# A graph attention layer: high softmax planes on ScalarE, weight remainders on GpSimd in quarters, q2 stacks straight from PSUM, five planes and a later value product

## The chip, the cores and the metric

The kernel runs on one core of a Trainium2 chip, in one launch. The metric is the device time of one execution in microseconds. Three executions of the kernel before gave a median of 329.63 us (328.7 to 329.89); one more was profiled. TensorE is called PE here, VectorE DVE, ScalarE ACT, GpSimd POOL and SyncE SP, as in the profile.

## The reference

```python
h = relu(layernorm(x))                       # x: 384 x 1024
q, k, v = h @ wq.T + bq, h @ wk.T + bk, h @ wv.T + bv
q2, k2, v2 = q @ wiq.T + biq, k @ wik.T + bik, v @ wiv.T + biv   # 16 heads of 64
scores = q2 @ k2.T / 8 + mask                # per head 384 x 384, mask from 6528 edges
attn = softmax(scores)
out = x + (attn @ v2).reshape(384, 1024) @ wo.T + bo
```

All is float32. The mask holds a weight by edge type where there is an edge, the weight of the fourth type on the diagonal where there is none, and minus infinity elsewhere.

## The kernel before, in words

**Numbers in two parts.** A value is held as a high part (rounded to the matrix format by a copy on ACT or DVE) and a remainder (value minus high part). A product is three matmuls, high by high, high by remainder, remainder by high (`mm3`, lines 373 to 375). A chunk of a weight matrix is a tile `raw` of 128 x 1024, loaded by SP (`load`, line 68); `split_hi` (line 80) writes its high part into `whl`, `split_lo` (line 85) the remainder, on DVE or POOL.

**Stages.** To about 150 us: layernorm, the projections v, q, v2 (kept as three bf16 parts in `vhl`) and k, and beside them the edge mask, gathered in `ma`. From about 161 us: the attention loop. It has a step `i` for each block of 128 queries of each head, so three steps for a head and six for a pair of heads `p`; 48 steps give scores, and some more finish. Two generators fill PE's time between: `fill_qk` computes q2 and k2 of the next pairs (16 chunks of 24 matmuls), `fill_o` the output projection. `fill` hands them out by a credit of 7.9 or 8 per step, with 84 ahead of the loop.

**A step.** Everything is issued in the order in which it is written, on each engine in its queue (the order is manual). Step `i` issues in this order: half of the filling; `do_S(i)`, two matmuls into a score bank `s` (two banks); the other half; `do_ttr(i - 1)` on DVE (line 721), which adds the mask, writes `e` and the row's minimum of the negated scores, and so frees the bank; `do_low(i - 4)`; `do_exp(i - 2)` on ACT (line 725) with the row sum; `do_norm(i - 3)`; every third step the value product `do_A` (line 750, nine matmuls) `LA` + 2 steps behind the head's first scores; a step later `do_ao` (lines 760 and 761), and once per pair `do_aos` (lines 765 and 766); last the tasks of the filling (`qk_head`: load, split and evacuation of chunks).

**The softmax planes.** The normalized row, scaled by 32768, becomes two fp16 planes in a tile `pl`. `do_norm` computes the reciprocal of the sum on DVE (line 729), the factor (line 730) and the high plane (line 732) on POOL. `do_low` computes the low plane on DVE (line 737) from `e`, the factor and the high plane, and then issues one transposing DMA from SP (line 742) into `pt`, where `do_A` reads it. There are three `pl` tiles, five `e` tiles, and room for four heads in `pt`.

**q2 and k2 stacks.** `qk_done` evacuates a finished chunk: ACT writes the high part into `nat` (line 383), DVE the remainder (line 384). For the scores, a head's high and remainder are stacked on 128 partitions: four DMAs copy 64-partition parts from `nat` into `qs` (lines 570 to 573) for q2, four into `ks` (line 580) for k2. All come from SP except in the first pair, where ACT issues half of them.

**Weight remainders.** In `qk_head` POOL takes the odd chunks and DVE the even ones; in `wo_prep`, which prepares the last six output chunks, POOL takes four (`OPOOL`) and DVE two.

Of the kernel before, what the change touches and what calls it, by code (L numbers as in the profile page):

```python
# [8 lines left out]
F32 = mybir.dt.float32  # L9
F32R = mybir.dt.float32r  # L10
I32 = mybir.dt.int32
F16 = mybir.dt.float16
BF16 = mybir.dt.bfloat16
PSC = 32768.0
AF = mybir.ActivationFunctionType
OP = mybir.AluOpType

N, D, NT, KT, NP = 384, 1024, 3, 8, 8
# [7 lines left out]
def gnn_kernel(ctx: ExitStack, tc: tile.TileContext, x, edges, erows, etw, wq, wk, wv, wiq, wik, wiv, wo,  # L26
# [6 lines left out]
    nc = tc.nc  # L33
    const = ctx.enter_context(tc.tile_pool(name="const", bufs=1))
    big = ctx.enter_context(tc.tile_pool(name="big", bufs=1))
    wpool = ctx.enter_context(tc.tile_pool(name="wpool", bufs=4))
    work = ctx.enter_context(tc.tile_pool(name="work", bufs=2))
# [1 line left out]
    dram = ctx.enter_context(tc.tile_pool(name="dram", bufs=1, space=bass.MemoryType.DRAM))  # L39
    ctx.enter_context(tc.manual_schedule())  # L40

    EB = 5
    NTAB, RNG = 3, EC // 3
    JI = [0, 1, 3, 5, 8, 11, 14, RNG]
    WARM = (20, 6, 0)
# [4 lines left out]
    def gtile(tag):  # L50
        return big.tile([128, 2, KT, N], F32R, tag=tag, name=tag)
# [8 lines left out]
    raw, whl = {}, {}  # L60
# [18 lines left out]
        else:  # L79
            nc.scalar.activation(dst[0], raw[w], AF.Copy)  # L80

    def split_lo(w, eng=None):
        if w < NCH:
            hi, lo = whl[w]
            (eng or nc.vector).tensor_tensor(lo, raw[w], hi.bitcast(F32), OP.subtract)  # L85

    def split(w, lo_eng=None, dst=None, hi_dve=False):
        split_hi(w, dst, hi_dve)
        split_lo(w, lo_eng)


    G3 = gtile("g3")
# [2 lines left out]
    xn = [xall[:, (NT + t) * D:(NT + t + 1) * D] for t in range(NT)]  # L95
    ert = work.tile([128, N], F32, tag="e", name="er", bufs=EB)
    er = ert[:, :2 * EC].bitcast(I32)
# [7 lines left out]
    bc = const.tile([128, 40], F32, name="bc")  # L105
# [21 lines left out]
    ma = const.tile([128, NT, N], F32, name="ma")  # L127
    krow = dram.tile([EC, 128], F32, name="krow")
    zero = work.tile([128, N], F32, tag="e", name="zero", bufs=EB)
    mbt = {}  # L130

    def mask_consts():
# [45 lines left out]

    krt = work.tile([128, N], F32, tag="e", name="kr", bufs=EB)
    kf = ert[:, :2 * EC]  # L180
# [28 lines left out]
    def mask_base():  # L209
        for j in range(NT):  # L210
            d = work.tile([128, N], F32, tag="e", name="d", bufs=EB)
            nc.gpsimd.tensor_tensor(d[:, :128], ident, w8[:, 7:8].to_broadcast([128, 128]), OP.mult)
# [33 lines left out]
    hT = gtile("g1")  # L246
    lnt = work.tile([128, N], F32, tag="e", name="lnt", bufs=EB)
    var, negm, root, vq, inv, rstd = (lnt[:, c:c + NT] for c in (4, 8, 12, 16, 20, 24))
# [133 lines left out]
    def evac(ps, hi, lo, bias):  # L382
        nc.scalar.activation(hi, ps[:, :N], AF.Identity, bias=bias)
        nc.vector.scalar_tensor_tensor(lo, ps[:, :N], bias, hi.bitcast(F32), op0=OP.add, op1=OP.subtract)

    def evac_row(ps, hi, lo, bias):
        f = work.tile([128, N], F32, tag="e", name="f", bufs=EB)
        nc.vector.tensor_tensor(f, ps[:, :N], rrow, OP.mult)  # L388
        nc.scalar.activation(hi, f, AF.Identity, bias=bias)  # L389
        post.append(lambda: nc.vector.scalar_tensor_tensor(lo, f, bias, hi.bitcast(F32), op0=OP.add, op1=OP.subtract))  # L390

    w = 0
# [120 lines left out]
    for k in range(8):  # L513
        slot_head(w)
        hi, lo = whl[w]
# [43 lines left out]
    gps = {}  # L559

    def qk_done(w):
        n, p = chunks[w]
        q2 = nc.scalar if p == 0 else nc.sync
        nat = work.tile([128, 2, N], F32R, tag="nat", name="nat", bufs=2)
        evac(gps[w], nat[:, 0, :], nat[:, 1, :], bc[:, (3 if n == "iq" else 4) * 8 + p:(3 if n == "iq" else 4) * 8 + p + 1])
        nf = nat.bitcast(F32)
        if n == "iq":
            qs = work.tile([128, 2, N], F32R, tag="qs", name="qs")
            qf = qs.bitcast(F32)
            nc.sync.dma_start(qf[0:64, 0, :], nf[0:64, 0, :])  # L570
            q2.dma_start(qf[64:128, 0, :], nf[0:64, 1, :])
            nc.sync.dma_start(qf[0:64, 1, :], nf[64:128, 1, :])
            q2.dma_start(qf[64:128, 1, :], nf[64:128, 0, :])
            stacks["q", p] = qs
        else:
            ks = work.tile([128, 2, 2, N], F32R, tag="ks", name="ks")
            kf = ks.bitcast(F32)
            for o in range(2):
                for r in range(2):
                    (q2 if r else nc.sync).dma_start(kf[r * 64:(r + 1) * 64, o, :, :], nf[o * 64:(o + 1) * 64, :, :])  # L580
            stacks["k", p] = ks
# [3 lines left out]
    def run_tasks():  # L585
        while tasks:
            tasks.pop(0)()

    def qk_head(w):
        first = w - W0 < 3  # L590
        if not first:
            load(w + 5)
            split_hi(w + 2)
        if pendq:
            pendq.pop(0)()
        if 0 < w - W0 < NTAB:
            mask_select(w - W0)
        if first:
            split_hi(w + 2)
        split_lo(w + 2, nc.gpsimd if (w + 2) % 2 == PAR else None)  # L600
        if first:
            load(w + 5)
        if w == W0:
            mask_select(0)
# [18 lines left out]
    W0 = 32  # L623
    WO = NCH - 8

    LA = 7
    PRE, RATE, RATE_O, RATE_E = 84, 7.9, 8, 8
    WSTEPS = (37, 40, 42, 44, 47, 51)
    PAR, OPOOL, ODVE = 1, (2, 3, 4, 6), (2,)
# [6 lines left out]
    def wo_prep(k):  # L636

        dst = None
        if k == 4:
            otile[0] = gtile("g3").rearrange("p a k n -> p (a k n)")  # L640
        if 4 <= k < 7:
            g, b = otile[0], (k - 4) * 2048
            dst = (g[:, b:b + 1024], g[:, b + 1024:b + 2048])
        split(WO + k, nc.gpsimd if k in OPOOL else None, dst, k in ODVE)
        load(WO + k + 3)

    def xb_load():
# [24 lines left out]
    def flush_y():  # L672
        while ysums:
            ysum(ysums.pop(0))
# [28 lines left out]
            omm(*OT[a], k)  # L703
            yield 4

    st_ps, es, sts, pls, pts, avs, aof = {}, {}, {}, {}, {}, {}, {}
    S = 48

    def do_S(i):
# [13 lines left out]
    def do_exp(i):  # L723
        s = sts[i]
        nc.scalar.activation(es[i], es[i], AF.Exp, bias=s[:, 0:1], scale=-1.0, accum_out=s[:, 1:2])  # L725

    def do_norm(i):
        s = sts[i]
        nc.vector.reciprocal(s[:, 3:4], s[:, 1:2])  # L729
        nc.gpsimd.tensor_scalar(s[:, 2:3], s[:, 3:4], PSC, None, op0=OP.mult)  # L730
        pl = pls[i] = work.tile([128, 2, N], F16, tag="pl", name="pl", bufs=3)
        nc.gpsimd.tensor_tensor(pl[:, 0, :], es[i], s[:, 2:3].to_broadcast([128, N]), OP.mult)  # L732

    def do_low(i):
        h, t = divmod(i, 3)
        pl = pls.pop(i)
        nc.vector.scalar_tensor_tensor(pl[:, 1, :], es.pop(i), sts[i][:, 2:3], pl[:, 0, :], op0=OP.mult, op1=OP.subtract)  # L737
        if t == 0:
            ptt = work.tile([128, 2, NT, N], F32, tag="pt", name="pt") if h % 2 == 0 else pts[h - 1][1]
            pf = ptt.rearrange("p a k n -> p a (k n)")[:, h % 2, :].bitcast(F16)  # L740
            pts[h] = pf.rearrange("p (c n) -> p c n", c=6), ptt
        nc.sync.dma_start_transpose(pts[h][0][:, :, t * 128:(t + 1) * 128], pl.rearrange("p a n -> p (a n)"))

    def do_A(h):
        p, o = divmod(h, 2)
        ps = avs[h] = bank("a")
        pt = pts[h][0]
        for k in range(3):
            for c, v in ((k, 2 * o), (3 + k, 2 * o), (k, 4 + o)):
                nc.tensor.matmul(ps[:, :N], vhl[:, k, p, v:v + 2, :], pt[:, c, :],  # L750
                                 start=(k == 0 and c == k and v < 4), stop=(k == 2 and v >= 4))
# [19 lines left out]
    def fill(n):  # L771
        credit[0] += n
        while credit[0] > 0 and gens:
            try:
                c = next(gens[0])
            except StopIteration:
                gens.pop(0)
                continue
            if c == 0:
                credit[0] = 0.0  # L780
                return
            credit[0] -= c

    fill(PRE)
    wp = 2
    for i in range(S + LA + 4):
        now[0] = i
        r = RATE if len(gens) == 2 else RATE_O if i < S else RATE_E
        fill(r / 2)
        if i < S:  # L790
            do_S(i)
        fill(r / 2)
        if 0 <= i - 1 < S:
            do_ttr(i - 1)
        if 0 <= i - 4 < S:
            do_low(i - 4)
        flush_y()
        if 0 <= i - 2 < S:
            do_exp(i - 2)
        if 0 <= i - 3 < S:  # L800
            do_norm(i - 3)
        j = i - LA
        if j >= 2 and (j - 2) % 3 == 0 and (j - 2) // 3 < 16:
            do_A((j - 2) // 3)
        if j >= 3 and (j - 3) % 3 == 0 and (j - 3) // 3 < 16:
            do_ao((j - 3) // 3)
        if j >= 4 and (j - 4) % 6 == 3:
            do_aos((j - 4) // 3)
        run_tasks()
        if i == XSTEP:  # L810
            assert len(gens) < 2
            xb_load()
        if i in WSTEPS:
            wo_prep(wp)
            wready[wp] = i + 2
            wp += 1
# [57 lines left out]
```

## Time and profile before

| what | value |
|---|---|
| median of three executions | 329.63 us (328.7 to 329.89) |
| the profiled execution: its own time | 330.62 us |
| its span | 328.9 us |
| mean granted clock of PE | 0.969 |
| busy: PE, weight loads | 297.6 us (90%), 262.1 us (80%) |
| busy: DVE, ACT, POOL | 229.7 us (70%), 140.1 us (43%), 170.5 us (52%) |
| DMA | 64.56 MB, mean 196 GB/s |
| low plane on DVE (line 737) | 48 of 1127 ns mean; 611 least, 619 median, 2733 most |
| high plane on POOL (line 732), factor (line 730) | 48 of 828 ns; 48 of 229 ns |
| weight remainder, 128 x 1024: DVE, POOL | 1225 ns; 2385 ns |
| transposing DMA: issue on SP, to landing | 1212 ns median; 3.6 us median |

Busy time is the time in which an engine works on an instruction, without waits. A matmul that is held up counts as busy, so a busy PE need not be at its peak. Waits name the instruction whose end released the waiting one. The granted clock is the share of full speed that PE was given.

### The profile page before, as it was taken

How to read it: one execution, taken by the hardware profiler on the slowest of the kernel's cores; microseconds unless marked ns; L12 is line 12 of the kernel's file. 1: busy time of each engine (PE TensorE's matmuls, PEld its weight loads, DVE VectorE, ACT ScalarE, POOL GpSimd, SP SyncE). 2: the span in 40 equal slices, each digit the busy share in tenths (PEclk: the TensorE clock that was granted, in tenths of full speed). 3: DMA queues.
4: the chain of work that ended last, by engine and by line, in shares of the span. 5: the costliest groups of instructions: out<-in, count | busy, mean ns of one | idle time of the engine just before them, and what ended most of it. 6: DMA issues, size and time to landing. Idle time of an engine off the chain costs nothing.

```text
span 328.9 us, 4908 instructions
## 1 busy us (share of the span) xinstructions
PE 297.6 (90%) x1561; PEld 262.1 (80%) x1561; DVE 229.7 (70%) x498; ACT 140.1 (43%) x248; POOL 170.5 (52%) x214
## 2 busy tenths in 40 slices
PE   7999999999999999999899768879797987598895
PEld 6899999999888999999888658668485864376575
DVE  5959967677665368987776487776868687887514
ACT  4773533333222245644555445444354445243210
POOL 4855673748577856000554364746455567556310
PEclk9999999999999999999999999979797999879799
DMA  7898855453963665724899969797897979933505
GB/s 286 261 354 310 281 169 204 163 193 124 298 213 131 203 214 171 280 88 130 244 246 243 194 171 224 172 201 201 199 205 167 225 144 196 346 62 72 74 0 192
DMA packets 60777, 64.56 MB, mean 196 GB/s; under 512 B 43216, under 2 KB 46800, under 8 KB 60752
## 3 DMA queue, kind: packets, MB, share of 16 engines
q1 hardware_dynamic: 58368, 61.86, 68.7%
q0 software_dynamic: 2064, 1.80, 2.0%
q10 hardware_dynamic: 320, 0.59, 0.7%
q8 instruction: 12, 0.20, 0.3%
q14 instruction: 13, 0.11, 0.1%
HBM read 40.39 MB, written 4.97 MB: 138 GB/s over the span
## 4 chain that ended last, share of the span: by engine, by line
PE 41%; DMA 16%; DVE 13%; POOL 12%; issue 9%; ACT 6%; SPq 2%; POOLq 0%; DVEq 0%; ACTq 0%
DMA pt<-pl 10%; PE g L375 9%; PE g L373 9%; PE g L374 9%; POOL pl L732 6%; POOL whl L85 3%; DVE whl L85 2%; PE a L750 2%; DMA raw<-in_wiq_dram 2%; DMA qs<-nat 2%; DVE ma L243 2%; PE s L373 2%; PE s L375 2%; PE s L374 2%; POOL s L730 2%
## 5 line engine op out<-in xcount | busy, mean ns | idle before, releaser
L373 PE MATMUL g<-g,whl 128*128 128x384 f32 x312 | 106.6, 342 | 0.0
L375 PE MATMUL g<-g,whl 128*128 128x384 f32 x312 | 105.2, 337 | 1.0 <-POOL whl L85 1.0
L374 PE MATMUL g<-g,whl 128*128 128x384 f32 x312 | 104.9, 336 | 0.0
L230 POOL DMA_INDIRECT tab<-val,idx x51 | 59.0, 1156 | 35.8 <-DMA tab<-val,idx 10.5
L737 DVE SCALAR_TENSOR_TENSOR pl<-e,s,pl 128x384 f16<-128x384 f32 x48 | 54.1, 1127 | 33.1 <-POOL pl L732 33.1
L80 ACT ACTIVATE whl<-raw 128x1024 fp32r<-128x1024 f32 x51 | 53.5, 1051 | 31.2 <-PE g L375 21.1
L375 PEld LDWEIGHTS g<-g,whl 128*128 128x128 f32 x312 | 59.0, 189 | 1.6 <-POOL whl L85 1.6
L373 PEld LDWEIGHTS g<-g,whl 128*128 128x128 f32 x312 | 59.2, 190 | 0.9 <-issue 0.3
L374 PEld LDWEIGHTS g<-g,whl 128*128 128x128 f32 x312 | 59.1, 189 | 0.0
L85 DVE TENSOR_TENSOR whl<-raw,whl 128x1024 fp32r<-128x1024 f32 x41 | 50.2, 1225 | 10.1 <-ACT whl L80 10.1
L725 ACT ACTIVATE e<-e,s 128x384 f32<-128x384 f32 x48 | 29.4, 613 | 53.5 <-DVE s L721 53.4
L732 POOL TENSOR_TENSOR pl<-e,s 128x384 f16<-128x384 f32 x48 | 39.7, 828 | 17.1 <-DMA pt<-pl 13.6
L715 PE MATMUL s<-ks,qs 128*128 128x384 f32 x96 | 27.1, 364 | 16.7 <-DVE s L721 14.9
L85 POOL TENSOR_TENSOR whl<-raw,whl 128x1024 fp32r<-128x1024 f32 x11 | 26.2, 2385 | 29.4 <-ACT whl L80 28.7
L715 PEld LDWEIGHTS s<-ks,qs 128*128 128x128 f32 x96 | 16.5, 193 | 23.8 <-DVE s L721 20.9
L389 ACT ACTIVATE g<-f,bc 128x384 fp32r<-128x384 f32 x24 | 14.8, 618 | 48.4 <-DVE f L388 48.4
L730 POOL TENSOR_SCALAR s<-s 128x1 f32<-128x1 f32 x48 | 11.0, 229 | 46.4 <-DVE s L729 43.1
L750 PE MATMUL a<-pt,vhl 128*128 128x384 f16 x144 | 31.3, 371 | 1.3 <-issue 1.3
L721 DVE CUSTOM_DVE_ANT_0 e<-s,ma 128x384 f32<-128x384 f32 x48 | 25.9, 540 | 1.1 <-PE s L715 1.1
L750 PEld LDWEIGHTS <-vhl 128*128 128x128 bf16 x144 | 14.3, 110 | 15.1 <-issue 9.4
L388 DVE TENSOR_TENSOR f<-g,rrow 128x384 f32<-128x384 f32 x24 | 13.3, 554 | 14.0 <-PE g L375 13.9
L373 PE MATMUL g<-whl,g 128*128 128x512 f32 x35 | 15.1, 431 | 3.4 <-DVE g L667 3.4
(148 smaller groups left out, 390.2 us busy)
## 6 DMA issues: line engine op xcount, KB each, us to landing
ks<-nat SPq DMA_DIRECT2D x30, 192.0 KB, 5.4
raw<-in_wv_dram SPq DMA_DIRECT2D x8, 512.0 KB, 6.9
raw<-in_wq_dram SPq DMA_DIRECT2D x8, 512.0 KB, 3.4
raw<-in_wiv_dram SPq DMA_DIRECT2D x8, 512.0 KB, 3.3
raw<-in_wk_dram SPq DMA_DIRECT2D x8, 512.0 KB, 4.7
raw<-in_wiq_dram SPq DMA_DIRECT2D x8, 512.0 KB, 4.4
raw<-in_wik_dram SPq DMA_DIRECT2D x8, 512.0 KB, 5.1
raw<-in_wo_dram SPq DMA_DIRECT2D x8, 512.0 KB, 4.9
```

Of the source, the lines that this page charges most:

```text
L80: nc.scalar.activation(dst[0], raw[w], AF.Copy)
L85: (eng or nc.vector).tensor_tensor(lo, raw[w], hi.bitcast(F32), OP.subtract)
L230: nc.gpsimd.indirect_dma_start(out=tabs[c // RNG], out_offset=bass.IndirectOffsetOnAxis(ap=idx[:, c:c + 1], axis=0), in_=val[:, c:c + 1], ...
L373: nc.tensor.matmul(ps, lhi, rhi, start=first, stop=False)
L374: nc.tensor.matmul(ps, lhi, rlo, start=False, stop=False)
L375: nc.tensor.matmul(ps, llo, rhi, start=False, stop=last)
L715: nc.tensor.matmul(ps[:, :N], qs[:, o, t * 128:(t + 1) * 128], ks[:, o, s, :], start=(s == 0), stop=(s == 1))
L721: nc.vector.tensor_tensor_reduce(e, st_ps.pop(i)[:, :N], ma[:, t, :], -0.125, 3.0e38, OP.add, OP.min, s[:, 0:1])
L725: nc.scalar.activation(es[i], es[i], AF.Exp, bias=s[:, 0:1], scale=-1.0, accum_out=s[:, 1:2])
L732: nc.gpsimd.tensor_tensor(pl[:, 0, :], es[i], s[:, 2:3].to_broadcast([128, N]), OP.mult)
L737: nc.vector.scalar_tensor_tensor(pl[:, 1, :], es.pop(i), sts[i][:, 2:3], pl[:, 0, :], op0=OP.mult, op1=OP.subtract)
L750: nc.tensor.matmul(ps[:, :N], vhl[:, k, p, v:v + 2, :], pt[:, c, :], start=(k == 0 and c == k and v < 4), stop=(k == 2 and v >= 4))
```

## The change

1. The factor (line 730 before) goes from POOL to DVE, and `do_norm` moves to the head of the softmax part of a step, ahead of `do_ttr`. The high plane becomes `do_high`, on ACT behind the step's exponential.
2. `split_lo` can work in parts. In `qk_head`, whose remainder is that of the chunk two later, POOL takes all from the seventh of the 16 chunks' heads on, and each is in four parts of 256 columns from the fifth on; in `wo_prep` POOL takes all six, in four parts.
3. For q2, ACT and DVE write `qs` straight from the bank, each in two instructions of 64 partitions; the four DMAs are gone. The program as built has the second instruction of ACT wait for the first of DVE.
4. There are five planes (three in the free part of the two `pt` tiles, two in a new tile `plx`) and six `e` tiles. `pt` holds three heads instead of four.
5. The transposing DMA is issued at the end of the step, behind the tasks (`do_turn`), and `LA` is 8 instead of 7, so that the value product comes a step later and the loop has one step more.

```diff
-    EB = 5
+    EB = 6
...
+            for j in range(parts):
+                c = slice(j * D // parts, (j + 1) * D // parts)
+                (eng or nc.vector).tensor_tensor(lo[:, c], raw[w][:, c], hi[:, c].bitcast(F32), OP.subtract)
...
         if n == "iq":
             qs = work.tile([128, 2, N], F32R, tag="qs", name="qs")
-            qf = qs.bitcast(F32)
-            nc.sync.dma_start(qf[0:64, 0, :], nf[0:64, 0, :])
-            q2.dma_start(qf[64:128, 0, :], nf[0:64, 1, :])
-            nc.sync.dma_start(qf[0:64, 1, :], nf[64:128, 1, :])
-            q2.dma_start(qf[64:128, 1, :], nf[64:128, 0, :])
+            for o in range(2):
+                m, l = slice(o * 64, o * 64 + 64), slice(64 - o * 64, 128 - o * 64)
+                nc.scalar.activation(qs[m, o, :], ps[m, :N], AF.Identity, bias=bias[m])
+                nc.vector.scalar_tensor_tensor(qs[l, o, :], ps[m, :N], bias[m], qs[m, o, :].bitcast(F32), op0=OP.add,
+                                               op1=OP.subtract)
             stacks["q", p] = qs
...
-        split_lo(w + 2, nc.gpsimd if (w + 2) % 2 == PAR else None)
+        split_lo(w + 2, nc.gpsimd if (w + 2) % 2 == PAR or w - W0 > 5 else None, 4 if w - W0 > 3 else 1)
...
-    LA = 7
+    LA = 8
...
-        split(WO + k, nc.gpsimd if k in OPOOL else None, dst, k in ODVE)
+        split(WO + k, nc.gpsimd, dst, k in ODVE, 4)
...
+    def pt_setup():
+        ts = [work.tile([128, 2, NT, N], F32, tag="pt", name="pt") for _ in range(2)]
+        f = [t.rearrange("p a k n -> p (a k n)").bitcast(F16) for t in ts]
+        c = 6 * N
+        ptv.extend(x.rearrange("p (c n) -> p c n", c=6) for x in (f[0][:, :c], f[0][:, c:], f[1][:, :c]))
+        plv.extend(f[1][:, c + 2 * N * j:c + 2 * N * (j + 1)].rearrange("p (a n) -> p a n", a=2) for j in range(3))
+        plv.extend(plx[:, j, :, :] for j in range(2))
+
     def do_norm(i):
         s = sts[i]
         nc.vector.reciprocal(s[:, 3:4], s[:, 1:2])
-        nc.gpsimd.tensor_scalar(s[:, 2:3], s[:, 3:4], PSC, None, op0=OP.mult)
-        pl = pls[i] = work.tile([128, 2, N], F16, tag="pl", name="pl", bufs=3)
-        nc.gpsimd.tensor_tensor(pl[:, 0, :], es[i], s[:, 2:3].to_broadcast([128, N]), OP.mult)
+        nc.vector.tensor_scalar(s[:, 2:3], s[:, 3:4], PSC, None, op0=OP.mult)
+
+    def do_high(i):
+        nc.scalar.activation(plv[i % 5][:, 0, :], es[i], AF.Copy, scale=sts[i][:, 2:3])
 
     def do_low(i):
+        pl = plv[i % 5]
+        nc.vector.scalar_tensor_tensor(pl[:, 1, :], es.pop(i), sts[i][:, 2:3], pl[:, 0, :], op0=OP.mult, op1=OP.subtract)
+
+    def do_turn(i):
         h, t = divmod(i, 3)
-        pl = pls.pop(i)
-        nc.vector.scalar_tensor_tensor(pl[:, 1, :], es.pop(i), sts[i][:, 2:3], pl[:, 0, :], op0=OP.mult, op1=OP.subtract)
...
-        nc.sync.dma_start_transpose(pts[h][0][:, :, t * 128:(t + 1) * 128], pl.rearrange("p a n -> p (a n)"))
+        nc.sync.dma_start_transpose(ptv[h % 3][:, :, t * 128:(t + 1) * 128], plv[i % 5].rearrange("p a n -> p (a n)"))
...
     for i in range(S + LA + 4):
...
+        if 0 <= i - 3 < S:
+            do_norm(i - 3)
         if 0 <= i - 1 < S:
             do_ttr(i - 1)
...
             do_exp(i - 2)
         if 0 <= i - 3 < S:
-            do_norm(i - 3)
+            do_high(i - 3)
...
         run_tasks()
+        if 0 <= i - 4 < S:
+            do_turn(i - 4)
```

More of the change, by code (lines that the diff above doesn't have):

```diff
@@ L80, in split_hi, with split_lo, split @@
             nc.scalar.activation(dst[0], raw[w], AF.Copy)
-    def split_lo(w, eng=None):
+    def split_lo(w, eng=None, parts=1):
         if w < NCH:
             hi, lo = whl[w]
-            (eng or nc.vector).tensor_tensor(lo, raw[w], hi.bitcast(F32), OP.subtract)
-    def split(w, lo_eng=None, dst=None, hi_dve=False):
+            for j in range(parts):
+                c = slice(j * D // parts, (j + 1) * D // parts)
+                (eng or nc.vector).tensor_tensor(lo[:, c], raw[w][:, c], hi[:, c].bitcast(F32), OP.subtract)
+    def split(w, lo_eng=None, dst=None, hi_dve=False, parts=1):
         split_hi(w, dst, hi_dve)
-        split_lo(w, lo_eng)
+        split_lo(w, lo_eng, parts)
     G3 = gtile("g3")
@@ L129, in gnn_kernel @@
     zero = work.tile([128, N], F32, tag="e", name="zero", bufs=EB)
+    plx = const.tile([128, 2, 2, N], F16, name="plx")
     mbt = {}
@@ L563, in qk_done @@
         q2 = nc.scalar if p == 0 else nc.sync
-        nat = work.tile([128, 2, N], F32R, tag="nat", name="nat", bufs=2)
-        evac(gps[w], nat[:, 0, :], nat[:, 1, :], bc[:, (3 if n == "iq" else 4) * 8 + p:(3 if n == "iq" else 4) * 8 + p + 1])
-        nf = nat.bitcast(F32)
+        ps, bias = gps[w], bc[:, (3 if n == "iq" else 4) * 8 + p:(3 if n == "iq" else 4) * 8 + p + 1]
         if n == "iq":
             qs = work.tile([128, 2, N], F32R, tag="qs", name="qs")
-            qf = qs.bitcast(F32)
-            nc.sync.dma_start(qf[0:64, 0, :], nf[0:64, 0, :])
-            q2.dma_start(qf[64:128, 0, :], nf[0:64, 1, :])
-            nc.sync.dma_start(qf[0:64, 1, :], nf[64:128, 1, :])
-            q2.dma_start(qf[64:128, 1, :], nf[64:128, 0, :])
+            for o in range(2):
[3 more added lines that the diff above has]
+                                               op1=OP.subtract)
             stacks["q", p] = qs
         else:
+            nat = work.tile([128, 2, N], F32R, tag="nat", name="nat", bufs=2)
+            evac(ps, nat[:, 0, :], nat[:, 1, :], bias)
+            nf = nat.bitcast(F32)
             ks = work.tile([128, 2, 2, N], F32R, tag="ks", name="ks")
@@ L704, in fill_o @@
             yield 4
-    st_ps, es, sts, pls, pts, avs, aof = {}, {}, {}, {}, {}, {}, {}
+    st_ps, es, sts, avs, aof = {}, {}, {}, {}, {}
+    ptv, plv = [], []
     S = 48
@@ L729, in do_norm @@
         nc.vector.reciprocal(s[:, 3:4], s[:, 1:2])
-        nc.gpsimd.tensor_scalar(s[:, 2:3], s[:, 3:4], PSC, None, op0=OP.mult)
-        pl = pls[i] = work.tile([128, 2, N], F16, tag="pl", name="pl", bufs=3)
-        nc.gpsimd.tensor_tensor(pl[:, 0, :], es[i], s[:, 2:3].to_broadcast([128, N]), OP.mult)
+        nc.vector.tensor_scalar(s[:, 2:3], s[:, 3:4], PSC, None, op0=OP.mult)
+    def do_high(i):
+        nc.scalar.activation(plv[i % 5][:, 0, :], es[i], AF.Copy, scale=sts[i][:, 2:3])
     def do_low(i):
+        pl = plv[i % 5]
+        nc.vector.scalar_tensor_tensor(pl[:, 1, :], es.pop(i), sts[i][:, 2:3], pl[:, 0, :], op0=OP.mult, op1=OP.subtract)
+    def do_turn(i):
         h, t = divmod(i, 3)
-        pl = pls.pop(i)
[L737 to L741, printed above, removed]
-        nc.sync.dma_start_transpose(pts[h][0][:, :, t * 128:(t + 1) * 128], pl.rearrange("p a n -> p (a n)"))
+        nc.sync.dma_start_transpose(ptv[h % 3][:, :, t * 128:(t + 1) * 128], plv[i % 5].rearrange("p a n -> p (a n)"))
     def do_A(h):
@@ L746, in do_A @@
         ps = avs[h] = bank("a")
-        pt = pts[h][0]
+        pt = ptv[h % 3]
         for k in range(3):
@@ L784, in gnn_kernel @@
     fill(PRE)
+    pt_setup()
     wp = 2
```

## The prediction

> **What bounds the kernel now.** I read the profile by stretches first, then the table of waits, then the timeline of one stretch. The stretches are cut at pairs of heads (six steps of the attention loop each). Columns: length, then busy time of PE, weight loads, DVE, ACT, POOL (instructions), granted clock, DMA share, GB/s.
>
> ```profile
> core 0: us, PE busy (x) PEld busy (x) DVE busy (x) ACT busy (x) POOL busy (x), PEclk, DMA share, GB/s
> ...
> 161.30:187.00 25.70, 23.57 (x133) 22.00 (x133) 16.35 (x45) 13.41 (x31) 11.68 (x17) 1.00 1.09 236
> 187.00:204.70 17.70, 12.85 (x72) 10.66 (x71) 12.79 (x28) 7.88 (x17) 9.50 (x14) 1.00 0.91 196
> 204.70:222.30 17.60, 14.33 (x72) 11.48 (x70) 12.65 (x30) 8.59 (x19) 9.49 (x14) 0.90 0.86 192
> 222.30:240.50 18.20, 15.98 (x82) 12.98 (x82) 12.93 (x30) 8.51 (x19) 9.49 (x14) 0.91 0.87 193
> ```
>
> Up to 156 us PE is busy 153.5 us of 156, so nothing is to be had there. From 187.0 to 295.8 us six pairs take 17.7, 17.6, 18.2, 17.7, 18.8 and 18.8 us, together 108.8. In them no engine is full: PE idles 20.1 us, and the clock is halved for 3.4 us at a time. From 187 to 312 us PE's idle time is 22.1 us and the halved clock (20.5 us at 0.5, up to 312) costs 10.2: 32.3 us is the most that a change to this loop can win.
>
> What makes a pair last 18 us is a ring of DVE and POOL. Waits (total us, times, longest):
>
> ```profile
> POOL s L730 <- DVE s L729: 43.1, 44, 3.4
> DVE pl L737 <- POOL pl L732: 33.1, 38, 3.8
> PEld s L715 <- DVE s L721: 20.9, 17, 3.0
> POOL pl L732 <- DMA pt<-pl: 13.6, 7, 4.1
> ```
>
> Each engine waits for the other, and PE waits for DVE's score reduction (L721), which frees the score bank. The timeline shows one turn:
>
> ```profile
> 223.95 2.36 POOL L85 TENSOR_TENSOR whl<-raw,whl 128x1024 fp32r<-128x1024 f32 x1
> 224.03 2.69 DVE L737 SCALAR_TENSOR_TENSOR pl<-e,s,pl 128x384 f16<-128x384 f32 x1 [1.21 <-POOL pl L732]
> 226.65 0.15 DVE L729 RECIPROCAL s<-s 128x1 f32<-128x1 f32 x1
> ...
> 226.88 0.21 POOL L730 TENSOR_SCALAR s<-s 128x1 f32<-128x1 f32 x1 [0.57 <-DVE s L729]
> 227.18 0.83 POOL L732 TENSOR_TENSOR pl<-e,s 128x384 f16<-128x384 f32 x1
> 228.04 0.62 DVE L737 SCALAR_TENSOR_TENSOR pl<-e,s,pl 128x384 f16<-128x384 f32 x1 [0.78 <-POOL pl L732]
> ...
> 228.82 0.21 POOL L730 TENSOR_SCALAR s<-s 128x1 f32<-128x1 f32 x1 [0.81 <-DVE s L729]
> ```
>
> L730 to L730 is 1.94 us: a step can't be shorter. And the low plane (L737), 0.62 us alone, takes 2.69 when a 2.36 us weight remainder of POOL (L85) stands beside it: it ends 0.41 us after that. A pair by this ring: 6 x 1.94 = 11.6; one such block 2.1; one behind POOL's remainder of the output (1.33 for 0.62) 0.7; on DVE a weight remainder 1.2, two evacuations (L384) 1.2, two L761 1.1. Sum 17.9 us, as measured. That is the bound; the transposes add to it where POOL waits for a free plane (13.6 us in 7 waits).
>
> **The change part by part, for one pair.**
>
> High planes and the factor. POOL loses 6 x (0.23 + 0.83) = 6.3 us, and the ring is cut: POOL is no longer between DVE's reciprocal and DVE's low plane. DVE gains six 128x1 multiplies. The trace has none on DVE; the nearest row is the reciprocal, 0.15 us, hidden down to 0.07 by overlap; as the multiply waits for the reciprocal's result I take 0.15, bounds 0.07 and 0.35. ACT gains six 128x384 passes with a per-row scale. Nearest rows: 0.52 (L765) and 0.62 (L725); I take 0.55. Added waits: the low plane now waits for ACT of the step before (behind it the evacuations and the next reduction), the factor heads DVE's step and waits for the exponential of the step before (behind it the reduction that frees PE's bank), and the high plane waits for the transpose of five planes ago (behind it the next exponential).
>
> Remainders in quarters. POOL does both of a pair: 2 x 2.4 us; from 1302 ns for 512 and 2385 for 1024 the fixed part is 0.22 us, so four quarters take some 3.0 us and POOL has 2 x 3.0 + 1.0 = 7.0 us a pair. It had 9.5; it isn't a bound. A remainder has two projections (6.7 us each) until PE needs it, and that covers it; without that cover it would cost 1.8 us (3.0 against 1.2 on DVE). DVE loses 1.2 us, and a block shrinks from 2.1 to at most a quarter, 0.75. Half of the time POOL works, so half of six low planes meet it, 0.4 us on average: 1.2 us. The new multiply heads DVE's step; I let it pass freely beside POOL, as the reciprocal in its place took 0.146 to 0.159 us in all 48 cases, though in the ring POOL mostly stood still then. [...]
>
> q2 stacks. Gone are four copies of 96 KB (4.1 us to land) and 2.3 us of SP's issuing; ACT does 2 x 0.49 for one 0.57, DVE 2 x 0.55 for one 0.62. In the built program ACT's second half waits for DVE's first; behind it stands the next exponential. I take 0.5 us on ACT; 0 to 2.
>
> Buffers and order. Five planes instead of three and a sixth e buffer: a plane has four steps instead of two before it is written again. In SP's queue the transpose is moved behind the step's weight load and K copies, so it waits for the K evacuation and up to 0.6 + 4 x 0.65 = 3.2 us of issuing. The A product comes one step later to cover this: at 2.4 us a step it has some 9.6 us for a transpose that lands in 3.6 (at most 6.7). SP's pair is 6 x 1.27 + 2 x 0.6 + 4 x 0.65 = 11.4 us, DMA's bytes fall from 3.4 to 3.0 MB, 12.6 us at the 236 GB/s seen at 161 to 187: both hidden under PE; without that cover a late transpose stops PE at A, by 1 us a pair if it lands at its longest.
>
> The new pair, engine by engine:
> PE: 47.4 projections at 0.17 (start to start), 12 scores at 0.175, 18 A products at 0.165: 13.3 us.
> DVE: 6 x (0.15 + 0.15 + 0.54 + 0.54) = 8.3; L761 1.1; evacuations 0.62 + 1.1; blocks 1.2: 12.3 (11 to 13.6).
> ACT: 6 x (0.71 + 0.55) = 7.6; L760 1.0; L765 0.5; weights 2 x 1.05; evacuations 0.57 + 1.0 + 0.5: 13.3 by durations, 12 where ACT's operations overlap (start to start they lie 0.1 closer).
>
> So PE comes next, with ACT and DVE just under it. With three engines at 90% and more that hand work to one another through two score banks I don't expect PE to run full: I add 1.1 us a pair, 14.4. No stall of over 2 us is left then that halves the clock. Between the ends, 13.3 and 16, this is nearer the lower, because from 161.3 to 184 us even the old ring ran ten steps at 2.24 us each, 13.4 a pair, while planes were free.
>
> Six pairs: 6 x 14.4 = 86.4 against 108.8: -22.4. Ahead of 187 us: -1 (0 to -2; the q copies ahead of the first scores). Behind 295.8 us: 0; PE is at 294 to 324 us nearly full, and one more step (2.2 us) of the loop is filled with products of the last weights; bounds -3.7 (idle 2.0, half clock 1.7) and +2.2. The profiled execution took 330.6 (span 328.9), 1.0 above the median of 329.6. 330.6 - 23.4 = 307.2; I say 307.
>
> **The rivals.**
> PE alone sets the pace: pairs of 13.3 us. -29, and up to 2 of the tail: 299 us. For it: the ten steps at 2.24. Against: ACT's sum is the same 13.3.
> ACT becomes the bound: if the high plane takes 0.8 (as the old one on POOL), and each handing over costs 0.2, a pair is 13.3 + 6 x 0.45 = 16 us: -12.8, 317 us. For it: ACT had 8.6 of 17.6 us and gets half as much again. Against: none of its 128x384 rows is above 0.62.
> The lock starves DVE: POOL's next quarter starts before the waiting low plane, so that quarters help nothing. Then a pair is DVE's 11.1 + 7.0 - 0.8 = 17.3, 103.8 for six: 325 us. For it: 2.69 us behind a whole remainder. Against: the low plane ended 0.41 us after POOL's instruction, at once; but no row has DVE waiting between two POOL instructions that follow each other.
> Slower: the ring comes back between DVE and ACT without overlap. Factor 0.3, reduction 0.54, exponential 0.71, high 0.55, low 0.54 and five handings over at 0.15 are 3.4 us a step; it decides from 3.02 us on (108.8 by 36). 36 x 3.4 = 122.4: +13.6, 344 us. For it: ACT and DVE are in order and cross twice in a step. Against: each crossing is laid one step apart, so that both can work at once.
> The loop is held by something that the change leaves alone: 0 us, for which no wait in the table speaks.
>
> **How the numbers follow.** Forecast (pairs of 13.8 to 15.2, 302 to 312 us): 0.55. PE alone 0.13, ACT 0.12, lock 0.08, slower 0.09, nothing 0.03. The range of 298 to 322 holds the first three, 0.80. Faster by over 0.5% (about what a measurement of this kernel can tell from no change): 0.55 + 0.13 + 0.12 + 0.08 = 0.88; the same 0.03; slower 0.09.
>
> **What would show it.** Right: no wait of DVE for POOL's plane; a pair (12 scores) in 14 to 15 us; L737's successor with no row over 1.4 us; no copies into qs; clock 1.00 from 187 us on; ACT and DVE at 80 to 90% there. Wrong: scores still waiting for L721's successor by 2 us and more (then DVE's row before says whether lock or ACT), A waiting for the transposes, or high planes over 0.7 us.

## The result

The changed kernel takes 315.72 us (median of four executions, 314.36 to 317.79) against 329.76 us for the kernel before, run beside it. The ratio is 0.957, with a 95% interval of 0.950 to 0.964. The profiled execution took 317.79 us, its span is 316.1 us. The forecast was 307 us, in a range of 298 to 322: the sign and the range held, but the time lies outside the 302 to 312 us of the forecast proper, and of the 23.4 us that the sum took off only about 14 came.

In the code after, the score reduction is line 726, the exponential 730, reciprocal and factor 742 and 743, the high plane 746, the low plane 750, the transposing DMA 754, the two halves of q2 572 (ACT) and 573 (DVE). First the stretches again, cut at the score reduction of each pair's last step; columns as in the prediction.

```profile
190.40:208.20 17.80, 15.30 (x79) 13.49 (x78) 11.06 (x37) 12.30 (x26) 6.95 (x9) 0.88 0.88 190
208.20:225.40 17.20, 15.22 (x79) 13.55 (x78) 10.98 (x36) 12.30 (x26) 6.95 (x9) 0.90 0.94 177
225.40:242.70 17.30, 15.33 (x79) 13.66 (x79) 11.10 (x37) 12.30 (x26) 6.94 (x9) 0.89 0.87 176
242.70:259.90 17.20, 15.22 (x79) 13.55 (x79) 11.03 (x37) 12.30 (x26) 6.96 (x9) 0.90 0.80 176
259.90:273.40 13.50, 13.50 (x66) 10.93 (x65) 10.80 (x36) 10.30 (x23) 7.25 (x9) 0.92 0.73 150
```

The first four pairs take 17.2 to 17.8 us, not 14.4. In them DVE works 11.0 us, ACT 12.3 and POOL 7.0, where the sum had 12.3, 12 to 13.3 and 7.0. PE is busy for 15.2 us, of which the half clock, one stretch of 3.4 us in each of these pairs, makes 1.7. So no engine has more work than forecast; they wait. The fifth pair, in the last line, is the first in which no q2 is written: it takes 13.5 us, and PE is busy all through it. The sixth takes 16.3 us. The waits (total us, times, longest):

```profile
DVE qs L573 <- ACT qs L572: 26.2, 14, 4.4
ACT qs L572 <- PE s L720: 13.4, 6, 3.2
PEld s L720 <- DVE s L726: 11.7, 7, 2.8
ACT qs L572 <- DVE qs L573: 7.7, 8, 2.9
ACT plx L746 <- DMA pt<-plx: 2.4, 2, 1.9
```

The waits of DVE for POOL's plane (33.1 us) and of POOL for DVE (43.1) are gone, as forecast. In their place stands a chain that begins at the write of q2. The timeline of one pair shows it, ACT first, then DVE, then PE:

```profile
234.26 1.04 ACT L80 ACTIVATE whl<-raw 128x1024 fp32r<-128x1024 f32 x1
237.89 0.58 ACT L572 ACTIVATE qs<-g,bc 64x384 fp32r<-64x384 f32 x1 [2.59 <-PE s L720]
239.15 0.58 ACT L572 ACTIVATE qs<-g,bc 64x384 fp32r<-64x384 f32 x1 [0.68 <-DVE qs L573]
239.75 0.61 ACT L730 ACTIVATE e<-e,s 128x384 f32<-128x384 f32 x1
...
238.50 0.61 DVE L573 SCALAR_TENSOR_TENSOR qs<-g,bc,qs 64x384 fp32r<-64x384 f32 x1 [3.74 <-ACT qs L572]
240.77 0.56 DVE L726 CUSTOM_DVE_ANT_0 e<-s,ma 128x384 f32<-128x384 f32 x1
...
237.33 0.52 PE L720 MATMUL s<-ks,qs 128*128 128x384 f32 x2
241.39 0.91 PE L720 MATMUL s<-ks,qs 128*128 128x384 f32 x2 [1.97 <-DVE s L726]
```

There are two `qs` buffers. The q2 chunk of a pair is finished one step before the last scores of the pair two before, which read the buffer that it goes into. Before the change ACT wrote q2 into `nat`, 1.2 to 1.7 us ahead of the end of those scores and without a wait for them; only the four DMAs in SP's queue wrote `qs`, and they were issued 0.2 to 3.8 us behind that end. Now ACT's instruction itself waits for the scores (until 237.85; all six of its waits end with the last score matmul of a pair), DVE's first half waits for ACT (3.74 us), the next reduction stands behind it on DVE, and PE waits 1.97 us for the score bank.

By the 48 score reductions: the first came at 163.5 us (162.0 before), reductions 11 to 47 took 99.3 us (107.0), and behind the last one came 26.4 us (30.5). The loop gave 7.7 us where 22.4 were forecast, the stage before it 2.5 less 1.5, the tail 4.1.

### The profile page after: what moved, and what is told of

It reads as the page before. It is cut to its first block, busy times and chain, and to the rows that moved or that the text cites. A ratio compares the mean times of both kernels' runs of the same rounds, so it can differ in the third digit from the quotient of the medians.

```text
span 316.1 us, 4808 instructions
## 1 busy us (share of the span) xinstructions
PE 293.2 (93%) x1561; PEld 265.4 (84%) x1561; DVE 213.0 (67%) x550; ACT 170.4 (54%) x304; POOL 146.2 (46%) x176
## 5 line engine op out<-in xcount | busy, mean ns | idle before, releaser
L376 PE MATMUL g<-g,whl 128*128 128x384 f32 x312 | 108.2, 347 | 0.0
L378 PE MATMUL g<-g,whl 128*128 128x384 f32 x312 | 106.9, 343 | 1.2 <-POOL whl L87 1.2
L377 PE MATMUL g<-g,whl 128*128 128x384 f32 x312 | 106.8, 342 | 0.0
L87 POOL TENSOR_TENSOR whl<-raw,whl 128x256 fp32r<-128x256 f32 (+1 forms) x59 | 49.9, 878 | 87.5 <-ACT whl L80 78.1
L233 POOL DMA_INDIRECT tab<-val,idx x51 | 56.3, 1103 | 37.7 <-DMA tab<-val,idx 12.9
L378 PEld LDWEIGHTS g<-g,whl 128*128 128x128 f32 x312 | 60.4, 194 | 1.5 <-POOL whl L87 1.5
L376 PEld LDWEIGHTS g<-g,whl 128*128 128x128 f32 x312 | 60.5, 194 | 0.6
L377 PEld LDWEIGHTS g<-g,whl 128*128 128x128 f32 x312 | 60.5, 194 | 0.0
L87 DVE TENSOR_TENSOR whl<-raw,whl 128x1024 fp32r<-128x1024 f32 (+1 forms) x38 | 43.2, 1142 | 10.5 <-ACT whl L80 10.5
L573 DVE SCALAR_TENSOR_TENSOR qs<-g,bc,qs 64x384 fp32r<-64x384 f32 x16 | 9.8, 616 | 26.3 <-ACT qs L572 26.2
L726 DVE CUSTOM_DVE_ANT_0 e<-s,ma 128x384 f32<-128x384 f32 x48 | 26.4, 550 | 0.4
L762 PE MATMUL a<-pt,vhl 128*128 128x384 f16 x144 | 26.2, 327 | 0.3 <-ACT plx L746 0.3
L746 ACT ACTIVATE pt<-e,s 128x384 f16<-128x384 f32 x30 | 18.4, 613 | 11.3 <-ACT e L730 5.9
L391 DVE TENSOR_TENSOR f<-g,rrow 128x384 f32<-128x384 f32 x24 | 13.3, 554 | 14.3 <-PE g L378 14.3
L750 DVE SCALAR_TENSOR_TENSOR pt<-e,s,pt 128x384 f16<-128x384 f32 x30 | 20.9, 697 | 0.0
L572 ACT ACTIVATE qs<-g,bc 64x384 fp32r<-64x384 f32 x16 | 9.2, 575 | 21.1 <-PE s L720 13.4
```

Of the source, the lines that this page charges most:

```text
L87: (eng or nc.vector).tensor_tensor(lo[:, c], raw[w][:, c], hi[:, c].bitcast(F32), OP.subtract)
L233: nc.gpsimd.indirect_dma_start(out=tabs[c // RNG], out_offset=bass.IndirectOffsetOnAxis(ap=idx[:, c:c + 1], axis=0), in_=val[:, c:c + 1], ...
L376: nc.tensor.matmul(ps, lhi, rhi, start=first, stop=False)
L377: nc.tensor.matmul(ps, lhi, rlo, start=False, stop=False)
L378: nc.tensor.matmul(ps, llo, rhi, start=False, stop=last)
L726: nc.vector.tensor_tensor_reduce(e, st_ps.pop(i)[:, :N], ma[:, t, :], -0.125, 3.0e38, OP.add, OP.min, s[:, 0:1])
```

## The experiments

Theory W: the direct write of q2 waits for the last scores of the pair two before and holds ACT, DVE and PE. Rivals: the four halves in series (H), DVE held by POOL's remainders (L), the DMA traffic (D). All ratios below are against the kernel before, run beside it on the same chip. Experiments 1 to 4, 5 to 8 and 9 to 12 ran on three chips, where its median was 330.33, 330.36 and 331.17 us, so across these groups the ratios are the ones to compare.

**1. The q2 evacuation two steps later.** Nothing else is changed; it then stands behind the scores that it waited for.

```diff
         if pendq:
-            pendq.pop(0)()
+            done = pendq.pop(0)
+            if now[0] >= 0 and chunks[w - 1][0] == "iq":
+                due.append((now[0] + 2, done))
+            else:
+                done()
...
         run_tasks()
+        while due and due[0][0] <= i:
+            due.pop(0)[1]()
```

> The changed kernel, with the q2 evacuations of the loop issued two steps later, behind the last scores of the pair that held the same qs buffer. Theory W (the direct write into qs by ACT waits for those last scores, 13.4 us in 6 waits, and holds ACT, then DVE, then PE): the wait is gone, and with it PE's 2.0 to 2.5 us of idle time a pair and most of the five half-clock stretches of 3.4 us; 296 to 305 us. Rival H (what costs is that the four half writes go ACT, DVE, ACT, DVE in series): they still do; 313 to 317 us. Rival L (DVE is held by POOL's remainders): nothing moves; 314 to 317 us.

Measured: 311.48 us, ratio 0.943 (0.938 to 0.947), against 0.957 (0.950 to 0.964). W's wait is gone, no stretch at half clock is left (granted clock 1.00 from 187 to 300 us), and the first four pairs take 15.2 to 16.9 us. H and L fall as causes of this wait. But W's figure was too bold: 311 and not 296 to 305. The waits of this kernel name what is next:

```profile
ACT plx L750 <- DMA pt<-plx: 6.0, 3, 3.2
ACT pt L750 <- DMA pt<-pt: 3.0, 2, 2.1
...
SPq L584 <- DVE s L747: 17.3, 5, 4.2
```

ACT's high plane (line 750 here) waits 9.0 us for planes to come free, and SP stands 17.3 us at the K copies (line 584), which wait for DVE, with the transposes queued behind them.

**2. q2 through DMA again, in the changed kernel.** The four copies out of `nat` come back in place of the two half writes on each engine.

> The changed kernel, with q2 evacuated into nat and copied into qs by four DMAs as before. Theory W: the wait for the last scores is SP's again, ACT and DVE are free; SP issues 2.3 us a pair more; 300 to 310 us, within 6 us of the kernel with late evacuation. Rival D (the copies were a burden of the queue, and their removal is where the gain came from): slower than the changed kernel, 318 to 326 us.

Measured: 313.29 us, ratio 0.946 (0.941 to 0.951). D falls: the removal of the copies brought nothing by itself. It also misses W's range by 3 us, though it is within 6 us of experiment 1. ACT has no wait for scores, and SP's queue a single one of 0.9 us, but ACT waits 24.2 us in 13 for planes. That the copies bring this about, by what they take of SP's queue ahead of the transposes, is a reading; no run tests it alone.

**3. The direct write alone, in the kernel before.** The edit is the part of the change in `qk_done`.

> The kernel before, with the direct write of q2 alone. Theory W: ACT waits for the last scores here too, and the wait falls into the ring of DVE and POOL; 1 to 2.5 us a pair, 336 to 345 us. Rival D: transposes land sooner, POOL waits less for planes; 322 to 329 us.

Measured: 332.39 us, ratio 1.0041 (1.0002 to 1.0081). ACT's wait for the scores is there (8.8 us in 6), and DVE's for ACT (12.8 us in 14), but both theories missed the size. DVE's wait for POOL's plane falls in turn, from 33.1 to 25.4 us (from 156 to 310 us), which fits a new wait that lies mostly inside the old one.

**4. Whole remainders on POOL**, with the late evacuation.

```diff
-        split_lo(w + 2, nc.gpsimd if (w + 2) % 2 == PAR or w - W0 > 5 else None, 4 if w - W0 > 3 else 1)
+        split_lo(w + 2, nc.gpsimd if (w + 2) % 2 == PAR or w - W0 > 5 else None, 1)
...
-        split(WO + k, nc.gpsimd, dst, k in ODVE, 4)
+        split(WO + k, nc.gpsimd, dst, k in ODVE, 1)
```

> The changed kernel with late evacuation, with POOL's remainders whole (128 x 1024, 2.4 us) instead of in quarters. If DVE's low plane waits for a whole POOL instruction and DVE has little slack: two blocks of up to 2.1 us a pair instead of about 0.4; 3 to 12 us above the kernel with late evacuation and quarters. If the slack of the planes and score banks hides a block of 2 us: within 2 us of it.

Measured: 312.89 us (312.27 to 314.11), ratio 0.946 (0.941 to 0.950): 1.4 us above experiment 1 (311.03 to 312.15), inside the 2 us that slack was given. Low planes of up to 2.80 us are back in this trace, and all 48 take 49.1 us instead of 34.6, so the block is there; PE's path has room for most of it. With late evacuation the quarters are not where the gain is. Whether they matter once the planes come free in time was not tested.

**5. Transposes ahead of the tasks**, on top of experiment 1.

```diff
+        if 0 <= i - 4 < S:
+            do_turn(i - 4)
         run_tasks()
...
-        if 0 <= i - 4 < S:
-            do_turn(i - 4)
```

> Late evacuation of q2, and the transposing DMA issued ahead of the step's tasks instead of behind them, so that in SP's queue it no longer stands behind the K copies, which wait for DVE (17.3 us in 5 waits with late evacuation alone). Theory P (what is left is held by planes that come free late: ACT's high plane waits 9.0 us in 5 waits for transposes): those waits go, 303 to 308 us against 311.5. Rival A (the order of work between ACT and DVE holds the pair at 15.9 us, and the planes only take up the slack): within 2 us of 311.5.

Measured: 306.90 us, ratio 0.929 (0.922 to 0.936). ACT's waits for planes fall from 9.0 us in 5 to 5.3 in 4, and the time by 4.6 us. P holds: what is left depends on when planes come free, though the waits are not all gone.

**6. Three planes instead of five**, on top of experiment 1 (`plv[i % 5]` becomes `plv[i % 3]`, three times).

> Late evacuation of q2, but three planes in turn instead of five. Theory P: ACT waits for a transpose in most steps, as POOL did before; 318 to 328 us against 311.5. Rival A: 311 to 315 us.

Measured: 335.27 us, ratio 1.014 (1.006 to 1.023): slower than the kernel before, and beyond P's range. From 162 to 290 us ACT waits 35.0 us in 8 for transposes, each time for that of three steps before.

**7. The high planes on ACT alone, in the kernel before.** The factor goes to DVE at the head of the step, as in the change; three planes stay.

```diff
-        nc.gpsimd.tensor_scalar(s[:, 2:3], s[:, 3:4], PSC, None, op0=OP.mult)
+        nc.vector.tensor_scalar(s[:, 2:3], s[:, 3:4], PSC, None, op0=OP.mult)
+
+    def do_high(i):
         pl = pls[i] = work.tile([128, 2, N], F16, tag="pl", name="pl", bufs=3)
-        nc.gpsimd.tensor_tensor(pl[:, 0, :], es[i], s[:, 2:3].to_broadcast([128, N]), OP.mult)
+        nc.scalar.activation(pl[:, 0, :], es[i], AF.Copy, scale=sts[i][:, 2:3])
```

> The kernel before, with the high planes on ACT and the factor on DVE at the head of the step, and nothing else: three planes, copies of q2, whole remainders, A seven steps behind. Theory R (the ring of DVE and POOL was the bound): the ring is gone and a pair falls from 17.8 to 16 to 17 us; 316 to 323 us. Rival P (three planes hold whichever engine writes them): 325 to 331 us.

Measured: 334.12 us, ratio 1.011 (1.004 to 1.018). Both missed: cutting the ring alone makes the kernel slower. The waits tell why, here of ACT and DVE from 162 to 290 us:

```profile
ACT pl L734 <- DMA pt<-pl: 34.7, 13, 4.0
...
DVE aof L763 <- ACT aot L762: 31.3, 11, 4.3
DVE nat L384 <- ACT nat L383: 15.9, 12, 4.6
```

The wait for a free plane was POOL's, 13.6 us. On ACT it is 34.7 us, and behind it stand the exponentials and the evacuations, for which DVE waits.

**8. ACT's two q2 halves ahead of DVE's two**, on top of experiment 5.

> As the kernel with late evacuation and early transposes, and both of ACT's q2 halves issued ahead of both of DVE's, so that ACT's second no longer waits for DVE's first (4.8 us in 7 waits, and DVE for ACT 6.9 us in 13). If these hand-overs are on PE's path: 2 to 5 us below that kernel; if they lie in slack: within 1.5 us of it.

Measured: 306.28 us, ratio 0.928 (0.921 to 0.934), as experiment 5: these hand-overs lie in slack.

**9. The ring, with planes enough.** As experiment 5, but factor and high plane on POOL in their place of before, and the remainders shared as before (POOL's in quarters).

> Five planes, late evacuation of q2, early transposes, remainders shared between DVE and POOL as before (POOL's in quarters), and the factor and the high plane back on POOL, at their place of before: the ring of DVE and POOL with planes enough. Ring theory: 6 x 1.94 us and DVE's other work in series; with the block of a remainder 0.4 instead of 2.1 us some 16.5 us a pair, 313 to 320 us. Theory P alone (planes were everything, the ring only looked like the bound): 305 to 310 us, as its partner with the high planes on ACT.

Measured: 324.07 us, ratio 0.978 (0.975 to 0.981). It is 4 us above the ring theory's range and 14 above the other's. The waits of the ring are back, from 162 to 290 us as large as in the kernel before (37.9, and 29.5):

```profile
POOL s L747 <- DVE s L746: 41.8, 30, 3.6
DVE pt L754 <- POOL pt L750: 19.4, 17, 2.6
DVE plx L754 <- POOL plx L750: 10.2, 8, 2.1
```

Its partner is experiment 10. The first four pairs take 17.2 us, where 16.5 were expected; the rest is not settled, though ACT's second q2 half waits 30.1 us in 7 here for DVE's first.

**10. The remainders shared as before**, on top of experiment 5: even chunks and two output chunks on DVE.

> Late evacuation and early transposes (306.9 us), with the weight remainders shared as before: even chunks and two of the output chunks on DVE whole, POOL's in quarters. DVE gets one remainder of 1.2 us a pair back. If DVE is on PE's path: 1.2 us in each of five pairs and 2.4 us behind them, 309 to 316 us. If it has slack: within 2 us of 306.9.

Measured: 314.89 us, ratio 0.949 (0.944 to 0.954), against 0.929 (0.922 to 0.936) for experiment 5. Giving DVE 5 x 1.2 + 2.4 us of work costs about 7 us by the ratios, and 8.0 by the times, which are of two chips. Three stretches of 3.4 us at half clock are back (mean granted clock 0.984, against 1.000 in experiment 5) and may be part of this cost. So moving the remainders to POOL is a large part of the gain in that kernel, and the ring (9 against 10, on one chip) costs another 9.2 us.

**11. Transposes ahead of the tasks alone**, in the changed kernel.

> The changed kernel with the transposing DMA ahead of the tasks, and the q2 evacuation where the change has it. Theory W (ACT waits for the last scores of the pair two before, at the evacuation): the wait is still there and the pair is held at about 17 us as in the changed kernel; 312 to 316 us. Theory P alone (planes): most of the way to 306.9 us, 307 to 310.

Measured: 316.70 us, ratio 0.956 (0.951 to 0.960): as the changed kernel, 0.7 us above W's range, with four pairs of 17.2 to 17.7 us and ACT's wait for scores 13.4 us in 6. The same edit that brings 4.6 us behind experiment 1 brings nothing while W's wait is there.

**12. Six planes**, on top of experiment 8, paid for with the sixth `e` tile.

```diff
-    EB = 6
+    EB = 5
...
-    plx = const.tile([128, 2, 2, N], F16, name="plx")
+    plx = const.tile([128, 3, 2, N], F16, name="plx")
...
-        plv.extend(plx[:, j, :, :] for j in range(2))
+        plv.extend(plx[:, j, :, :] for j in range(3))
```

`plv[i % 5]` becomes `plv[i % 6]`.

> Late evacuation, early transposes, ACT's halves first (306.3 us), with six planes instead of five and five e tiles instead of six. Theory P, further: ACT's waits for transposes (7.5 us in 6) go, 302 to 305 us. If five e tiles hold DVE's reduction instead: 306 to 310 us.

Measured: 301.62 us (301.21 to 302.92), ratio 0.911 (0.908 to 0.914): the fastest, 14 us below the changed kernel and just below P's range. Four of its pairs (the other two take 14.3 and 16.3 us):

```profile
184.20:198.70 14.50, 14.13 (x81) 12.12 (x80) 11.77 (x36) 12.30 (x26) 7.35 (x10) 1.00 1.05 213
198.70:213.30 14.60, 14.07 (x81) 12.08 (x80) 11.72 (x36) 12.30 (x26) 7.37 (x10) 1.00 1.15 219
213.30:227.90 14.60, 13.95 (x80) 11.97 (x79) 11.66 (x36) 12.31 (x26) 7.32 (x10) 1.00 0.93 200
227.90:242.50 14.60, 13.46 (x77) 11.46 (x76) 11.65 (x36) 12.30 (x26) 7.32 (x10) 1.00 1.02 218
```

ACT's 12.3 us are those of the changed kernel. What differs is that PE is busy for 13.5 to 14.1 of 14.6 us, at full clock, and DMA moves 200 to 219 GB/s instead of 176 to 190. ACT has no wait for a transpose left in the loop. It has five `e` tiles, as the kernel before: here the sixth was not needed.

## Why the prediction was right or wrong

**What held, and what was luck.** The sign came through what the sum had taken off, the ring, and what it had added, the planes. The range held in part by luck. The pair that it was built on came at 17.2 us, above the 16 that was its upper end; the time is inside because the tail gave 4.1 us that were set at 0, and because the fifth pair, with no q2 to write, took 13.5. Of the signs set down beforehand these came: no wait of DVE for POOL's plane, no low plane over 1.4 us (1.18 at most), no copies into `qs`. These did not: pairs of 14 to 15 us, the clock at 1.00, ACT and DVE busy at 80 to 90% (72% and 64%). And the sign of being wrong came: scores wait up to 2.5 us for the reduction, behind which stands neither a DVE instruction lengthened beside POOL nor ACT's work, but a wait of ACT.

**The bound before.** The ring was real: with planes enough, putting it back costs 9.2 us (9 against 10). It was not the whole bound. I set the 13.6 us that POOL waited for planes beside the ring as an addition; experiments 6 and 7 show that with three planes, cutting the ring is a loss of 1%. The change works because it does both, and my sum had both, but its reason named one.

**The term that was mis-sized: the q2 stacks.** I took 0.5 us a pair on ACT, 0 to 2, and looked for the wait in the program between ACT's halves. That one was small (0.7 us each in the loop, and in slack by experiment 8). The wait that counts is the one for the `qs` buffer, which the step of moving work from a DMA to an engine carried along: what had cost SP's queue no wait, as the copies came behind the scores, stands now in ACT's queue ahead of them, with the exponentials behind it. It held four pairs at 17.2 us and more; moved out of the way (experiment 1) they take 15.2 to 16.9, while moving the transposes alone (experiment 11) leaves them as they were.

**"No stall of over 2 us is left that halves the clock."** Wrong for the changed kernel (five stretches), right once the wait is gone: none at all in experiments 1, 5 and 12 before the last matmuls (granted clock 1.00 from 187 to 300 us). In the trace before, the half clock came five times from 187 to 312 us, four times for 3.4 us and once for 6.8, each time within 1.5 us of the end of a gap of PE of 2.01 to 3.44 us; after one of 2.66 us, at 195.6 us, it did not come. That such gaps bring it was an estimate of mine, and 2 us is no limit: in the changed kernel it came behind gaps of 1.97 and 1.98 us too.

**Transposes behind the tasks.** I hid them under PE and priced a late one as a stop of PE at A. In the changed kernel A never waits for a transpose. A late transpose stops ACT at the high plane instead: 2.4 us in the changed kernel, where the q2 wait covered it, 9.0 us once that was gone. Experiments 5 and 12, in which planes come free earlier, bring 4.6 and about 5 us.

**The 1.1 us for handing over.** With both waits away (experiment 12) four pairs take 14.6 us, where the sum had 14.4. It came by other terms: PE's three terms add up to 13.1 us, not to the 13.3 that is printed, and PE is busy for 13.5 to 14.1. The span there is 29.4 us below that of the kernel before: 18.1 between reductions 11 and 47, 4.2 in the step from reduction 10 to 11, 3.0 ahead of it and 4.1 behind the last. So the loop gave about the 22.4 us that were forecast, the stage ahead of it 2 more than its 1, and the tail, set to 0 between -3.7 and +2.2, gave 4.1, in the changed kernel too. The trace before has a gap of PE of 2.0 us and a stretch of 3.4 us at half clock there, and the traces of the changed kernel and of experiment 12 have neither.

**Parts that came as priced.** Factor 0.154 us (0.15), high plane 0.616 us (0.55, the row of 0.62 was the nearer), a quarter 0.74 us (0.75), busy times of ACT and POOL as above; DVE's came 1.3 us lower. The low planes lost less to POOL's quarters: 48 of them took 33.0 us, 3.7 over 48 x 0.611, so 0.5 us a pair instead of 1.2; none was over 1.18 us. The two q2 halves cost as much as whole instructions (0.576 on ACT, 0.616 on DVE, against 0.573 and 0.613 for 128x384 in lines 383 and 384 before; I took 0.49 and 0.55, as in the 64x384 rows of lines 760 and 761, 0.487 and 0.546).

**The rivals.** The rival that the forecast calls the lock, in which POOL's next quarter starts before DVE's waiting low plane and holds it again, did not come: the longest low plane of the changed kernel (1.18 us, at 270.30 us) ended 0.41 us behind the quarter beside it, while POOL's next one, of 1.06 us instead of 0.74, was still running. ACT as the bound came in time (317) but not in its mechanism: ACT is busy 12.3 us of 17.2. PE alone at 13.3 us a pair is what the changed kernel shows in its fifth pair only. The slower case did not come in the changed kernel. In experiment 7 ACT and DVE do wait for one another, but behind ACT's waits for planes, so its mechanism is not shown there either.

**What stays open.** The later A product was never tested alone, nor the sixth `e` tile in the changed kernel; the move of the remainders was tested only with late evacuation and early transposes, where it counts for much.

## What to carry to other kernels

When a copy by DMA is replaced by a direct write, the dependence on the destination buffer moves into the queue of the engine that writes, and can become a wait there (here 13.4 us of ACT in 6): ask who reads that buffer last, and place the write behind it. Count the buffers between an engine and a slow transfer by the transfer's whole way, its place in the queue included (here six planes left ACT no wait, five left 5 to 9 us of it, three 35.0); with too few, moving work to another engine only moved the wait, and to a busier queue (13.6 us on POOL before, 34.7 on ACT in experiment 7). When busy times are as forecast and the time isn't, follow the waits back to the first engine that waits, here ACT, before adding capacity.

## What the runs showed of the hardware

In the changed kernel's loop PE's granted clock fell to half for 3.4 us five times, each time within 1.1 us of the end of an idle gap of PE of 1.97 to 2.5 us (1.97 at 239.4 us). After one gap of 2.02 us, at 172.6 us, it did not fall, and with late evacuation, where PE's longest wait was 1.7 us (experiment 1) or 1.4 (experiment 5), the granted clock was 1.00 from 187 to 300 us.

The 128x1 multiply on DVE took 0.152 to 0.155 us in all 48 cases of the changed kernel, 12 of which lie wholly inside an elementwise instruction of POOL. In the fastest kernel four quarters run on POOL while it passes:

```profile
225.54 3.15 POOL L87 TENSOR_TENSOR whl<-raw,whl 128x256 fp32r<-128x256 f32 x4 [1.04 <-ACT whl L80]
...
225.56 1.14 DVE L756 SCALAR_TENSOR_TENSOR pt<-e,s,pt 128x384 f16<-128x384 f32 x1
...
227.85 0.15 DVE L749 TENSOR_SCALAR s<-s 128x1 f32<-128x1 f32 x1
```

The low plane, started beside a quarter, takes 1.14 us, where 0.61 is its least; the multiply is not held, here or in any of the 48 cases of this run (0.153 to 0.157 us).
